# Attention's gate loads issued behind the spread reciprocals, and their bias added to x in the projection's step

## The chip, the cores and the metric

The kernel runs on one core of a Trainium2 chip. The metric is the device time in microseconds of one execution. PE is TensorE's matmul stream (PEld its weight loads), DVE is VectorE, ACT is ScalarE, POOL is GpSimd, and SP is SyncE, which here does nothing but issue DMAs. Each engine works through its own instructions in order and waits where an operand is not ready. All DMAs in the part studied here are issued on SP's queue, so a DMA that waits for its source also holds back every DMA issued behind it.

## The reference

The input x has 128 batches of 64 tokens and 128 channels, in float32. There are four blocks; only the first three use the code in question. A self-attention with 16 heads of 8 channels, its output scaled by a gate per batch and channel, is (shortened):

```python
qkv = (modulate(_ln(x), shift, scale) @ W_qkv + b_qkv)
attn = softmax(q @ k.T * HD ** -0.5)          # 16 heads, 64 x 64 per batch and head
x = x + gate[:, None] * ((attn @ v) @ W_proj + b_proj)
```

The first block (L0) runs a self-attention, a cross-attention with the context and an MLP; the second (L1) one cross-attention; the third (L2) again self-attention, cross-attention and MLP. The fourth (L3) is a small mixture of experts. A cross-attention has no gate: x = x + (attn @ v) @ W + b.

## The kernel before, in words

The 8192 tokens are cut into 16 groups of 512 (8 batches); `xs[s]` is the part of x that belongs to group s and stays in SBUF for the whole kernel. Attention is run as a hand-written software pipeline over groups: `attend` gets the list of all groups of several attentions in a row (L0 self then L0 cross, 32 in all; later L1 cross, L2 self, L2 cross, 48 in all), and `step(k)` issues one half group (4 batches) of each stage:

- `scores` (L459): 32 small matmuls into the one PSUM tile `sc`, then on DVE the row maxima `mx` (L476) and `e = sc - mx` (L478).
- `turned` (L484): transposes of e, and the exponential on ACT.
- `weighted` (L500): the product with v. Beside the 8 output channels of each head, columns of ones in `vbd` give the softmax's denominators, so the tile `o` holds outputs and sums.
- `prepare` (L377): a generator with eight parts for a coming group: loading the context c for cross-attentions (L385), the statistics, the normalization `xn` on POOL (L363), transposes, the storing of the transposed context `ctxT` in L0 cross (L411), k with its block-diagonal copy `kbd` on POOL (L435), q, v.
- `finish` (L521): a generator with four parts for a past group, which is where the change lies.

The four parts of `finish` for group j are issued in these steps: the first late in the second half step of group j+1, the second in the first half step of group j+2, the third in the second half step of group j+2, the fourth in the first half step of group j+3. They do this:

1. The denominators go to DRAM (`sums`, two DMAs, L529) and come back as a compact 128 x 64 tile (`rc`, L533). In a self-attention `gate_tile` (L272) then loads `gt` with two DMAs (L277): for each token the gate and the gate times the projection's bias, from a small table in DRAM, the row of a batch repeated for its 64 tokens. Four DMAs (L538) move the odd heads' outputs within `o`.
2. DVE takes the reciprocal of rc (L540); it goes to DRAM (`recs`, L542) and is read back spread over each head's 8 channels (`rb`, L544).
3. POOL forms `oT = o * rb` (L547) and adds the bias to x (L549): a row of biases in a cross-attention, the second half of gt in a self-attention.
4. PE projects oT (`py`, L553). In a cross-attention DVE adds py to x. In a self-attention DVE multiplies py by the first half of gt (`y`, L558), and POOL adds y to x (L559).

On each engine and on SP's queue the order is the order in which the Python code issues: in `step`, the second part of group i-2 comes before the fourth part of group i-3, and the first part of group i-1 before the third of group i-2. Tile pools with two buffers hold gt, rc and y; rb and oT have one. In the first self-attention, the `prepare` of L0 cross starts four groups before the end of the self groups, so that from then on SP also issues c, and somewhat later the stores of ctxT, between rb and the next group's sums; at the end of L2 self it is c alone.

Of the kernel before, what the change touches and what calls it, by code (L numbers as in the profile page):

```python
# [11 lines left out]
ALU = mybir.AluOpType  # L12
# [3 lines left out]
P = 128  # L16
NST = 16
TT = 4
# [41 lines left out]
def tile_kernel(ctx: ExitStack, tc: tile.TileContext, a: dict, out: bass.AP):  # L60
    nc = tc.nc
    V, S, G, T = nc.vector, nc.scalar, nc.gpsimd, nc.tensor
# [3 lines left out]
    def const(shape, name):  # L66
        return cp.tile(shape, F32, tag=name, name=name)
# [25 lines left out]
    xs = [const([P, TT, P], f"x{s}") for s in range(NST)]  # L93
# [91 lines left out]
    proj_bias = {}  # L185
# [86 lines left out]
    def gate_tile(pool, s, wp):  # L272

        gt = pool.tile([P, TT, 2, P], F32, tag="gt", name="gt")
        for h in range(2):
            r = gates[wp].rearrange("(s t h) i c -> s h t (i c)", t=TT, h=2)[s, h]
            nc.sync.dma_start(  # L277
                gt[ts(h, L)].rearrange("p t i c -> p t (i c)"),
                r.unsqueeze(0).broadcast_to([L, TT, 2 * P]),
            )  # L280
        return gt
# [239 lines left out]
    def finish(pools, at):  # L521

        pool, psum = pools[:2]
        s, o = at["s"], at["o"]
        cross = at["layer"][2] == "c"

        sums = dp.tile([16, NT], F32, tag="sums", name="sums", bufs=2)
        for j in range(2):
            nc.sync.dma_start(  # L529
                sums.rearrange("(g i j) t -> j g i t", i=2, j=2)[j], o[16 + j : P : 32, :, :]  # L530
            )
        rc = pool.tile([P, L], F32, tag="rc", name="rc")
        nc.sync.dma_start(rc, sums.rearrange("h (c t) -> (h c) t", t=L))  # L533
        if not cross:
            gt = gate_tile(pool, s, at["wp"])

        for g in range(4):
            nc.sync.dma_start(o[32 * g + 16 : 32 * g + 32, 0, :], o[32 * g : 32 * g + 16, 1, :])  # L538
        yield
        V.reciprocal(rc, rc)  # L540
        recs = dp.tile([16, NT], F32, tag="recs", name="recs", bufs=2)
        nc.sync.dma_start(recs.rearrange("h (c t) -> (h c) t", t=L), rc)  # L542
        rb = pool.tile([P, NT], F32, tag="rb", name="rb", bufs=1)
        nc.sync.dma_start(rb, recs.unsqueeze(1).broadcast_to([16, HD, NT]))  # L544
        yield
        oT = pool.tile([P, NT], F32, tag="oT", name="oT", bufs=1)
        G.tensor_tensor(oT, o[:, 0, :], rb, ALU.mult)  # L547
        bias = proj_bias[at["wp"]].unsqueeze(1).broadcast_to([P, TT, P]) if cross else gt[:, :, 1, :]
        G.tensor_tensor(xs[s], xs[s], bias, ALU.add)  # L549
        yield  # L550
        py = psum.tile([P, TT, P], F32, tag="mm", name="py")
        for t in range(TT):
            T.matmul(py[:, t, :], oT[:, ts(t, P)], w[at["wp"]][:, 0], start=True, stop=True)  # L553
        if cross:
            V.tensor_add(xs[s], xs[s], py)
        else:
            y = pool.tile([P, TT, P], F32, tag="y", name="y")
            V.tensor_tensor(y, py, gt[:, :, 0, :], ALU.mult)  # L558
            G.tensor_tensor(xs[s], xs[s], y, ALU.add)  # L559

    def attend(pools, ats):

        n = len(ats)
        prep = [prepare(pools, at) for at in ats]
        fin = [finish(pools, at) for at in ats]

        def go(gens, i):
# [708 lines left out]
```

## Time and profile before

| | |
|---|---|
| median of 3 runs | 1644.17 us (1642.24 to 1647.26) |
| the profiled execution's own time | 1646.88 us |
| its span | 1645.1 us |
| granted TensorE clock, mean | 0.996 |
| L0 self (first to last reciprocal) | about 49 to 233 us |
| L2 self (first to last reciprocal) | about 781 to 961 us |
| gate loads in attention | 64 DMAs of 256 KB |
| sums / rc / recs / rb | 160 of 16 KB / 80 of 32 KB / 80 of 32 KB / 80 of 256 KB |
| bias adds in self-attention, POOL L549 | 32 of 1278 ns |

The span is what the profiler saw between the first and the last instruction; the execution's own time is 1.8 us longer. The page gives for each group of instructions the engine, the line, the tiles as out<-in, the count, the busy time, the mean duration, and the idle time just before with what ended it. A timeline lists single instructions by start; a bracket behind one is the idle time before it and what released it.

### The profile page before, as it was taken

Reading aid. Unit: us, or ns where it says so; the run is one execution under the profiler, and the core shown is the slowest. Engines: PE = TensorE matmul, PEld = TensorE weight load, DVE = VectorE, ACT = ScalarE, POOL = GpSimd, SP = SyncE. Lnnn points to the kernel's source line nnn. Section 1 sums busy time; section 2 is a strip of 40 time slices with the busy share of each in tenths; the row PEclk is TensorE's granted clock in tenths of the full one; section 3 lists DMA queues with packets and bytes.
Section 4 is the critical chain, followed back from the end, with each engine's and each line's share of the span. In section 5 each row is a group of like instructions: output and inputs, shape, how many; then the busy total and the mean of one; then the engine's idle time right before and its main releaser. Section 6 shows DMA issues by size and latency. Waiting matters only on the chain.

```text
span 1645.1 us, 64937 instructions
## 1 busy us (share of the span) xinstructions
PE 1585.5 (96%) x27874; PEld 1094.6 (67%) x27874; DVE 1292.3 (79%) x2426; ACT 1029.8 (63%) x1696; POOL 1090.0 (66%) x1834
## 2 busy tenths in 40 slices
PE   6999999998999899999999999998999999999998
PEld 4677767776554477767777777776777666666665
DVE  7999989998576688899999999996453666666665
ACT  5788767776333587887878888885334444444442
POOL 5687777775899888977778776775866333334322
PEclk9999999999999999999999999999999999999999
DMA  7333443322202022222333432222432101111100
GB/s 207 83 95 85 104 117 89 92 80 61 61 27 59 26 60 62 61 52 56 85 91 86 109 86 73 62 59 55 127 81 74 39 30 36 39 34 38 31 13 16
DMA packets 145998, 112.70 MB, mean 69 GB/s; under 512 B 35573, under 2 KB 124463, under 8 KB 145711
## 3 DMA queue, kind: packets, MB, share of 16 engines
q1 hardware_dynamic: 145504, 108.53, 25.0%
q8 instruction: 219, 3.59, 1.0%
q14 instruction: 68, 0.56, 0.1%
q10 hardware_dynamic: 207, 0.03, 0.0%
HBM read 83.99 MB, written 14.02 MB: 60 GB/s over the span
## 4 chain that ended last, share of the span: by engine, by line
PE 75%; DVE 14%; POOL 3%; ACT 3%; DMA 2%; issue 2%; SPq 1%; POOLq 0%; DVEq 0%; ACTq 0%
PE sc L469 9%; PE pp L494 8%; PE po L511 7%; PE ph L1043 6%; PE ph L1044 6%; DVE mx L476 6%; DVE e L478 6%; PE ph L674 5%; PE po L1074 5%; PE psT L333 5%; PE pk L427 4%; PE py L553 4%; PE pvv L450 3%; PE py L691 3%; PE pq L440 3%; PE py L680 2%
## 5 line engine op out<-in xcount | busy, mean ns | idle before, releaser
L498 ACT ACTIVATE eT<-pp 128x1024 f32<-128x1024 f32 x320 | 329.6, 1030 | 165.4 <-PE pp L494 165.3
L476 DVE TENSOR_REDUCE mx<-sc 128x32 f32<-128x2048 f32 x160 | 366.5, 2291 | 59.7 <-PE sc L469 59.6
L478 DVE TENSOR_TENSOR e<-sc,mx 128x2048 f32<-128x2048 f32 x160 | 366.7, 2292 | 5.5
L494 PEld LDWEIGHTS pp<-ident,e 64*128 64x128 f32 x5120 | 185.2, 139 | 141.9 <-ACT eT L498 45.3
L435 POOL TENSOR_SCALAR kbd<-kT,mask 128x512 f32<-128x512 f32 x316 | 212.3, 689 | 38.5 <-ACT kT L429 35.6
L494 PE MATMUL pp<-ident,e 64*128 64x64 f32 x5120 | 229.0, 229 | 8.5 <-DVE e L478 4.7
L363 POOL TENSOR_SCALAR xn<-x,nmu,rs 128x128 f32<-128x128 f32 x508 | 220.0, 447 | 13.3
L547 POOL TENSOR_TENSOR oT<-o,rb 128x512 f32<-128x512 f32 x80 | 102.0, 1274 | 160.8 <-DMA rb<-recs 75.6
L469 PE MATMUL sc<-kbd,qT 32*64 32x256 f32 x5120 | 181.0, 390 | 16.5 <-DVE e L478 14.8
L675 ACT ACTIVATE h<-ph,vec 128x512 f32<-128x512 f32 x128 | 87.3, 687 | 157.8 <-PE ph L674 157.7
L511 PE MATMUL po<-eT,vbd 128*32 128x64 f32 x10240 | 178.5, 221 | 1.3 <-issue 0.8
L1050 ACT ACTIVATE h<-h 128x512 f32<-128x512 f32 x112 | 69.1, 628 | 160.0 <-DVE h L1046 131.9
L511 PEld LDWEIGHTS po<-eT,vbd 128*32 128x32 f32 x10240 | 151.8, 110 | 14.3 <-issue 1.3
L321 POOL TENSOR_TENSOR rs<-rs,nhalf 128x4 f32<-128x4 f32 x128 | 130.7, 1021 | 10.7
L469 PEld LDWEIGHTS sc<-kbd,qT 32*64 32x64 f32 x5120 | 98.2, 132 | 53.4 <-issue 19.3
L1046 DVE TENSOR_TENSOR h<-ph,ab 128x512 f32<-128x512 f32 x112 | 76.9, 687 | 64.6 <-PE ph L1044 64.4
L311 DVE BATCH_NORM_STATS2 st<-x 128x6 f32<-128x128 f32 x512 | 110.5, 279 | 1.0 <-DMA x<-in_x_dram 0.5
L1067 POOL TENSOR_SCALAR g<-g 128x512 f32<-128x512 f32 x16 | 10.0, 622 | 140.7 <-ACT g L1066 140.7
L1043 PE MATMUL ph<-nx,w 128*128 128x512 f32 x192 | 99.8, 601 | 0.0
L1074 PEld LDWEIGHTS po<-w_2o,h 128*128 128x128 f32 x768 | 92.2, 192 | 10.9 <-issue 8.4
L1079 DVE SCALAR_TENSOR_TENSOR acc<-po,pr,acc 128x128 f32<-128x128 f32 x192 | 67.2, 350 | 39.9 <-PE po L1074 35.3
L519 ACT COPY o<-po 128x512 f32<-128x512 f32 x160 | 95.7, 598 | 4.4 <-PE po L511 2.1
(259 smaller groups left out, 2954.7 us busy)
## 6 DMA issues: line engine op xcount, KB each, us to landing
rb<-recs SPq DMA_DIRECT2D x80, 256.0 KB
c<-in_ctx_dram SPq DMA_DIRECT2D x80, 256.0 KB
o<-o SPq DMA_DIRECT2D x320, 32.0 KB
gt<-gate_L_xcond_sa_proj_w SPq DMA_DIRECT2D x32, 256.0 KB
gt<-gate_L_xcond_W_proj SPq DMA_DIRECT2D x32, 256.0 KB
gt<-gate_L_xcond_W_mlp SPq DMA_DIRECT2D x32, 256.0 KB
x<-in_x_dram SPq DMA_DIRECT2D x16, 256.0 KB
ctxT<-cm SPq DMA_DIRECT2D x16, 256.0 KB
```

The source lines that it names most:

```text
L311: V.bn_stats(st[:, t, :], src[:, t, :])
L321: G.tensor_tensor(rs, rs, nhalf, ALU.pow)
L363: engine.tensor_scalar(xn[:, t, :], src[:, t, :], nmu[:, t : t + 1], rs[:, t : t + 1], ALU.add, ALU.mult)
L435: (V if at.get("first") else G).tensor_scalar(kbd[:, j], by_batch(kT), mask[:, j : j + 1], 1.0, ALU.mult, ALU.mult)
L469: T.matmul(sc[ts(h, L), g, ts(t2, 256)], qT[ts(g, 32), ts(b, L)], kbd[ts(g, 32), :, b, :], start=True, stop=True,)
L476: V.tensor_reduce(mx, sc.rearrange("p g (m k) -> p (g m) k", k=L), AX.X, ALU.max)
L478: V.tensor_tensor(e, sc.rearrange("p g (m k) -> p (g m) k", k=L), mx.unsqueeze(2).broadcast_to([P, 32, L]), ALU.subtract,)
L494: T.transpose(pp[:, h, ts(4 * g2 + 2 * i + t2, L)], e6[ts(h, L), 2 * gg + g2, t2, i], ident[ts(h, L), ts(h, L)],)
L498: S.activation(eT[:, gg], pp, AF.Exp, scale=HD ** -0.5)
L511: T.matmul(po[ts(g, 32), i, ts(2 * t2 + h, L)], at["vbd"][:, 4 * u + 2 * t2 + h, 2 * g + i, :], e7[:, g // 2, h, g % 2, i, t2, :], start=T ...
L1043: T.matmul(ps, wn, d["nx"], start=True, stop=False)
L1074: T.matmul(po[:, ex, :], d[q][:, ts(t, P)], k3["w_2o"][:, q, :], start=r == 0, stop=r == 1)
```

## The change

In self-attention groups two things move, and nothing is added or removed. The call of `gate_tile`, and with it the two DMAs of gt, moves from the first part of `finish` (behind rc, ahead of the moves within o) to the end of the second part (behind rb). The bias add on POOL moves from the third part (behind oT) to the fourth, where it is issued after the projection's matmuls and ahead of y. Cross-attentions are unchanged.

```diff
         nc.sync.dma_start(rc, sums.rearrange("h (c t) -> (h c) t", t=L))
-        if not cross:
-            gt = gate_tile(pool, s, at["wp"])
 
         for g in range(4):
...
         nc.sync.dma_start(rb, recs.unsqueeze(1).broadcast_to([16, HD, NT]))
+        if not cross:
+            gt = gate_tile(pool, s, at["wp"])
         yield
         oT = pool.tile([P, NT], F32, tag="oT", name="oT", bufs=1)
         G.tensor_tensor(oT, o[:, 0, :], rb, ALU.mult)
-        bias = proj_bias[at["wp"]].unsqueeze(1).broadcast_to([P, TT, P]) if cross else gt[:, :, 1, :]
-        G.tensor_tensor(xs[s], xs[s], bias, ALU.add)
+        if cross:
+            bias = proj_bias[at["wp"]].unsqueeze(1).broadcast_to([P, TT, P])
+            G.tensor_tensor(xs[s], xs[s], bias, ALU.add)
         yield
...
         else:
+            G.tensor_tensor(xs[s], xs[s], gt[:, :, 1, :], ALU.add)
             y = pool.tile([P, TT, P], F32, tag="y", name="y")
             V.tensor_tensor(y, py, gt[:, :, 0, :], ALU.mult)
```

## The prediction

> **What bounds the kernel now.** The page first. TensorE is busy 96% of the span, and nearly the whole chain of work that ended last runs over PE and DVE in attention. No queue heads the list, so the question is where a queue reaches into that chain.
>
> ```profile
> PE 1585.5 (96%) x27874; PEld 1094.6 (67%) x27874; DVE 1292.3 (79%) x2426; ACT 1029.8 (63%) x1696; POOL 1090.0 (66%) x1834
> PE 75%; DVE 14%; POOL 3%; ACT 3%; DMA 2%; issue 2%; SPq 1%; POOLq 0%; DVEq 0%; ACTq 0%
> ```
>
> Second, the timeline of a quiet stretch of the first self-attention (columns: start, duration, engine, line, operation).
>
> ```profile
> 157.06 0.54 DVE L540 RECIPROCAL rc<-rc 128x64 f32<-128x64 f32 x1
> 157.63 0.33 SPq L542 DMA_DIRECT2D recs<-rc  x1
> 160.93 0.56 SPq L544 DMA_DIRECT2D rb<-recs  x1
> 161.62 1.17 SPq L529 DMA_DIRECT2D sums<-o  x2
> 164.37 1.28 POOL L547 TENSOR_TENSOR oT<-o,rb 128x512 f32<-128x512 f32 x1 [2.45 <-DMA sums<-o]
> 164.78 0.33 SPq L533 DMA_DIRECT2D rc<-sums  x1
> 165.25 1.30 SPq L277 DMA_DIRECT2D gt<-gate_L_xcond_sa_proj_w  x2
> 166.60 2.50 SPq L538 DMA_DIRECT2D o<-o  x4
> 168.98 0.54 DVE L540 RECIPROCAL rc<-rc 128x64 f32<-128x64 f32 x1
> ```
>
> One group takes 11.92 us (reciprocal to reciprocal, 157.06 to 168.98). DVE sets it: twice a 2.29 us maximum and a 2.29 us subtraction, with PE's 1.12 us of scores between. The reciprocal (0.54) and y (0.63) just fill one such gap, so a reciprocal that waits for rc lengthens the group nearly one for one. SP closes a loop beside this: reciprocal, recs, rb, the next group's sums, rc, next reciprocal. Here it has slack.
>
> Third, DVE's timeline and the chain of waits later in the same stage, where SP also loads c and stores ctxT for the next layer: there the slack is gone.
>
> ```profile
> 206.59 0.55 DVE L540 RECIPROCAL rc<-rc 128x64 f32<-128x64 f32 x1 [1.19 <-DMA rc<-sums]
> 219.47 0.55 DVE L540 RECIPROCAL rc<-rc 128x64 f32<-128x64 f32 x1 [1.28 <-DMA rc<-sums]
> 233.06 0.55 DVE L540 RECIPROCAL rc<-rc 128x64 f32<-128x64 f32 x1 [1.78 <-DMA rc<-sums]
> ...
> PEld py L553 <- POOL oT L547: 5.7, 4, 2.4
> DVE rc L540 <- DMA rc<-sums: 5.0, 4, 1.8
> ```
>
> The reciprocals stand at 192.82, 206.59, 219.47, 233.06 and 245.85: 53.0 us for four groups instead of 47.7. These 5.3 us are nearly all that SP's order can win.
>
> **The change, part by part.**
>
> *Bias add on POOL.* The 32 adds of 1.28 us (40.9 us busy) stay, later in POOL's order: removed between oT and the two rs operations, placed between kbd and the add of y. Behind the old place rs moves up 1.28 us; behind the new one the add of y, nmu and four xn slip by as much, then oT. Kbd ends near 158.7; two adds of 1.28 and 1.9 us of nmu and xn end at about 163.2, while oT waits for rb until 164.37 anyway (the 2.45 us idle). xn is read a group later, x by the next layer sixteen groups later. Cost zero; the cover is that idle time. Without it (126.44, oT idle only 0.47) oT slips up to 1.28, PE's py still has more than that in hand, and the price is at most a few tenths.
>
> *The two gate DMAs.* Their bytes (0.52 MB a group) and number are unchanged; they leave the place between rc and the o moves and go behind rb. What leaves: 1.3 to 2.3 us of SP issue ahead of the o moves, and the gate's data ahead of recs. Readers of gt (the bias add and y of the fourth part) come about 12.4 us after the reciprocal, gt lands by about 9 (issued at 3 to 5, and the lone load below takes 3.8 from issue to its last data): no wait. What arrives: behind gt on SP now stand c, ctxT and, above all, the next sums, on which rc and the DVE reciprocal depend. The work on DVE, PE and ACT is untouched.
>
> How long does gt hold the rings? Nearest row: the windows of one gate load alone, in the last MLP.
>
> ```profile
> 1268.00:1268.50 0.50, 0.50 (x17) 0.43 (x13) 0.00 (x0) 0.00 (x0) 0.00 (x0) 1.00 0.19 68
> 1268.50:1269.00 0.50, 0.50 (x2) 0.26 (x3) 0.43 (x2) 0.00 (x0) 0.00 (x0) 1.00 0.95 336
> 1269.00:1270.00 1.00, 1.00 (x8) 0.76 (x7) 0.42 (x1) 0.36 (x1) 0.00 (x0) 1.00 1.11 234
> 1270.00:1271.00 1.00, 1.00 (x6) 0.66 (x6) 0.00 (x0) 0.33 (x1) 0.00 (x0) 1.00 0.48 89
> ```
>
> The last two columns are DMA share and GB/s: about 2.5 us of data. The Trainium skill (DMA: Bandwidth & Descriptors, "Anatomy of one DMA — SWDGE (gpsimd) path") puts data at bytes over 436e3 per us behind about 2 us of fixed cost, for another issue path: 1.2 us for 0.52 MB. I take the row for the rings. The price of gt ahead of sums then lies between 1.3 (issue alone) and 2.5 us in a full queue.
>
> The SP loop afterwards, from one reciprocal's start to the next:
> - to recs: 0.57 (157.06 to 157.63).
> - recs to rb: 1.5 to 3.3 before; by the queue's timeline the mean is 2.4 in groups with gates and 2.0 in L1 cross, which has none. Gates now come later: 2.0.
> - rb to issue of rc: not shown with gt in it; bounded below by 3.85 (160.93 to 164.78, no gt), above by 3.85 + 2.5. The nearest row has the same 0.77 MB behind rb's start: rb, c and ctxT at 198.12, rc at 203.75, so 5.6. Taken.
> - rc to the reciprocal it releases: 2.84, 1.85 and 2.28 (rc at 203.75, 217.62, 230.78): 2.3.
>
> Sum 10.5, against 11.92: in the mean hidden, slack 1.4. The parts scatter by about 0.9 us together (estimate from the ranges above), so a group now and then overshoots; the mean overshoot is some 0.05 us. By kind of group:
> - 20 groups with no load in their way (ten in each self-attention): 20 x 0.05 = +1.0.
> - Six at the end of the second self-attention and two in the first, with c: 0.8 more, 11.3; overshoot about 0.13: +1.0.
> - Four with c and ctxT: 0.6 + 2.3 (o moves still right ahead of recs) + 5.7 + 2.0 for gt (between 1.3 and 2.5) + 2.3 = 12.9, against 53.0/4 = 13.26: -1.4. What wins here is that recs no longer stands behind gt and o moves (reciprocal 206.59, recs only 209.08, rb 212.04); what eats it is gt ahead of sums. With the page's 1.2 us of data the issue's 1.3 would set the term, the loop would be 12.2 and the four groups would win 4.2.
>
> Sum +0.6 us: 1647.5 against the profiled execution's own 1646.88 (span 1645.1 plus 1.8 around it). That execution lies 2.7 us above the median of the three runs, so against 1644.17 it is 1644.8. With the page's figure it would be about 1642.
>
> **The rivals.** *Slower: the reciprocal waits for gates.* One mechanism: gt ahead of sums on SP and in the rings, paid at the DVE reciprocal. It decides from the point where rb to rc exceeds 7.0 us, because then the quiet loop passes 11.92. At 7.1 (1.5 more than taken) the quiet groups have about 0.4 us each (8), the eight with c about 0.9 (7), the four late ones 14.4 against 13.26 (4.6): +20, 1664. At half that excess, about +7, 1651. For: rc already waits late in the first self-attention with no gt in the way, gate issues stretch from 1.3 to 2.3 us, gate rows are small pieces read many times. Against: the quiet loop's 1.4 us.
>
> *Faster: the late groups come free.* If recs lands in 1.5 and gt costs only its issue, the late loop is 0.6 + 1.5 + 7.0 + 1.9 = 11.0, below 11.92, and the 5.3 us go: 1638.9. For: PE's 5.7 us of waiting on oT there comes from a late rb, and rb moves up. Against: rb, gt, c and ctxT are then 1.3 MB in a row, with sums behind them.
>
> *Nothing happens at all:* the bias half is that; the DMA half would be if the waits just change places. It is inside the main case.
>
> **How the numbers follow.** About 0.3% (4.9 us) is what a measurement of this kernel can tell from no change. Main case, loops as summed: 0.50, of which 0.39 within the bound, 0.04 faster, 0.07 slower (each part is a small difference of large terms). Slower rival 0.34: 0.29 slower, 0.05 within. Faster rival 0.16: 0.13 faster, 0.03 within. Together: faster 0.17, same 0.47, slower 0.36. Range: from the faster rival's 1638 to between the slower one's half and full price, 1657; the main case's own is 1640 to 1650.
>
> **What would show it.** Right: in quiet stretches sums starts about 0.4 us later after the reciprocal than 4.56 now, rc to reciprocal shrinks from 4.2–4.9 us towards 3, without a DVE wait for rc; recs to rb falls towards 2.0; late in the first self-attention recs follows the reciprocal within about 0.6–1 us instead of 2.5, rb to rc grows from 5.7 to about 7.7, the period there is about 12.9; oT's wait for rb does not grow. Wrong: DVE waits for rc in most of the 32 groups (slower rival); no DVE wait for rc late in the first self-attention (faster); a wait of y or of the bias add for gt; oT or xn late because of POOL's new order.

## The result and the profile after

The changed kernel takes 1657.15 us (median of 6 runs, 1655.15 to 1660.71) against 1643.33 for the kernel before in the same series (1640.6 to 1647.26): ratio 1.0084, 95% interval 1.0066 to 1.0103. It is slower by about 14 us, where the forecast's likeliest case was no change. The profiled execution of after has a span of 1655.4 us, 10.3 more than before's 1645.1. The traces can explain these 10.3 us; the rest of the 13.8 is that before's profiled execution lay above its own median.

The page of after: busy times as before, but more of the chain runs through DMA.

```profile
PE 1585.6 (96%) x27874; PEld 1094.1 (66%) x27874; DVE 1292.3 (78%) x2426; ACT 1031.3 (62%) x1696; POOL 1091.0 (66%) x1834
PE 74%; DVE 14%; DMA 4%; ACT 3%; POOL 3%; issue 2%; SPq 1%; POOLq 0%; DVEq 0%; ACTq 0%
```

No engine works more than 1.5 us longer (PE 1585.5 before, 1585.6 now); the DMA share of the chain went from 2% to 4%. So the loss is waiting. The same quiet stretch as was shown of before, by the timeline (start, duration, engine, line, operation; the lines have shifted with the edit: L538 is the reciprocal, L540 recs, L542 rb, L529 sums, L533 rc):

```profile
159.16 0.54 DVE L538 RECIPROCAL rc<-rc 128x64 f32<-128x64 f32 x1
159.73 0.33 SPq L540 DMA_DIRECT2D recs<-rc  x1
162.62 0.56 SPq L542 DMA_DIRECT2D rb<-recs  x1
163.23 1.30 SPq L277 DMA_DIRECT2D gt<-gate_L_xcond_sa_proj_w  x2
164.64 1.15 SPq L529 DMA_DIRECT2D sums<-o  x2
169.12 0.32 SPq L533 DMA_DIRECT2D rc<-sums  x1
171.32 0.55 DVE L538 RECIPROCAL rc<-rc 128x64 f32<-128x64 f32 x1 [0.16 <-DMA rc<-sums]
```

From rb to rc it is 6.50 us here (before: 3.85), and of that the sums' own round trip, from their issue to rc's, is 4.48 (before, 161.62 to 164.78: 3.16). The slack is used up: the bracket shows DVE beginning to wait for rc.

SP's own waits over the first ten groups (49 to 170 us) say the same. Before, then after (total us, times, longest):

```profile
SPq L533 <- DMA sums<-o: 13.9, 11, 1.8
SPq L529 <- ACT qT L442: 13.6, 9, 2.4
...
SPq L533 <- DMA sums<-o: 24.9, 11, 3.0
SPq L529 <- ACT qT L442: 5.4, 6, 1.9
```

On average SP waits 1 us longer for sums to land before it can issue rc. The second row shows something else: in quiet groups sums does not start as soon as rb is issued, but when ACT has copied o (the row names qT, which ACT runs right behind that copy). In before this was about 4.5 us after the reciprocal, whether rb had come 1.5 or 3.3 us after recs. So an earlier rb gains nothing on the way to rc in a quiet group. The issue of the gates mostly falls into that wait, and what they add shows in the time from sums to rc.

Where SP also loads c the loop no longer fits. DVE's timeline in the stretch that follows, and the whole run's row in the chain of waits (total us, times, longest):

```profile
184.94 0.55 DVE L538 RECIPROCAL rc<-rc 128x64 f32<-128x64 f32 x1 [1.78 <-DMA rc<-sums]
199.78 0.55 DVE L538 RECIPROCAL rc<-rc 128x64 f32<-128x64 f32 x1 [3.24 <-DMA rc<-sums]
212.62 0.54 DVE L538 RECIPROCAL rc<-rc 128x64 f32<-128x64 f32 x1
225.83 0.55 DVE L538 RECIPROCAL rc<-rc 128x64 f32<-128x64 f32 x1 [0.40 <-DMA rc<-sums]
239.35 0.55 DVE L538 RECIPROCAL rc<-rc 128x64 f32<-128x64 f32 x1 [1.90 <-DMA rc<-sums]
252.36 0.55 DVE L538 RECIPROCAL rc<-rc 128x64 f32<-128x64 f32 x1 [1.41 <-DMA rc<-sums]
...
DVE rc L538 <- DMA rc<-sums: 21.2, 12, 3.5
```

Before, that row read 12.2 us in 6 waits; now it is 21.2 in 12. In the two self-attentions alone it is 5.0 us in 4 waits before and 14.3 in 10 after; 8 of these 10 are in the 12 groups where c is also loaded. The chain of after through the longest of these waits shows what stands in it, one SP instruction behind the other (L277 the two gate loads, L385 c; pieces under 0.1 us are left out):

```profile
189.83 0.56 SPq L542
...
190.45 0.64 SPq L277
...
191.14 0.61 SPq L277
...
191.79 0.60 SPq L385
...
193.11 4.04 DMA sums<-o
...
197.20 2.49 DMA rc<-sums
```

The two gate issues take 1.3 us, and the second of the two 16 KB DMAs of sums behind them takes 4.04 us to land. In the group of the same place before, sums was issued 1.29 us after rb and rc 3.23 us after sums; here it is 2.66 and 4.71. The gates' issue and their data are both paid in one group.

A second loss was not foreseen. Three quiet groups lasted 12.88, 13.10 and 12.88 us without any DVE wait for rc. PE's timeline there shows a gap in the middle of a run of matmuls whose operands were ready, put down to no releaser:

```profile
108.73 0.60 PE L554 MATMUL py<-L_xcond_sa_proj_w,oT 128*128 128x128 f32 x3 [0.70 <-issue]
143.88 0.42 PE L511 MATMUL po<-eT,vbd 128*32 128x64 f32 x14 [0.90 <-issue]
879.35 0.53 PE L511 MATMUL po<-eT,vbd 128*32 128x64 f32 x21 [0.69 <-issue]
```

The same stretches of before have none of these. The most likely cause is PE's supply of instructions, for this reason. DMA queue 8, which the page calls `instruction`, brings blocks of 16 KB (219 of them, 3.59 MB), in the self-attentions one every 5.2 us in the median. In all the traces of this case together there are 33 gaps of PE's matmuls of over 0.3 us that have no releaser, and every one of them ends 1.2 to 1.6 us after such a block has landed. The three gaps above followed blocks that came 7.1, 6.9 and 7.7 us after the one before. The windows in which the block before the gap at 143.88 came show it at the end of the burst of rb and gt (the last two columns are the DMA share, where 1 is all 16 engines, and GB/s):

```profile
141.00:141.50 0.50, 0.50 (x21) 0.14 (x6) 0.23 (x4) 0.36 (x1) 0.50 (x1) 1.00 0.67 131
141.50:142.00 0.50, 0.50 (x16) 0.44 (x15) 0.47 (x1) 0.00 (x0) 0.33 (x3) 1.00 0.12 35
```

In the self-attentions of after ten blocks come over 6.5 us behind the last one, in before and in the kernel without gate loads none. That PE waits for a block in these gaps is thus well supported by the timing. That gt's burst is what delays the block is argued; gaps of about 1.0 to 1.2 us also stand in traces of kernels whose gates had not been moved (the bias add alone, c and ctxT on ScalarE's queue).

Stage by stage, from reciprocal to the same reciprocal in both traces:

| stage | before | after | difference | forecast |
|---|---|---|---|---|
| L0 self, ten quiet groups | 119.49 | 121.87 | +2.4 | +0.5 |
| L0 self, two with c | 23.84 | 28.46 | +4.6 | +0.25 |
| L0 self, four with c and ctxT | 53.03 | 52.58 | -0.45 | -1.4 |
| L2 self, ten quiet groups | 119.20 | 121.92 | +2.7 | +0.5 |
| L2 self, six with c | 73.73 | 75.95 | +2.2 | +0.75 |

The sum is +11.5, of which about 1.2 comes back later (the spans differ by 10.3). Of the quiet groups' 5.1 the three gaps make 3.1 (12.88, 13.10 and 12.88, each less 11.92), and one group of L2 that overshoots (a 1.34 us wait for rc) most of the rest. One of the four late groups (from 199.78) also holds a short drop of the granted TensorE clock, 0.57 in the mean from 201.5 to 205.5, where before has 1.00 in all of both self-attentions; it lasted 12.84 us without a wait for rc, so the -0.45 is not the DMAs' order alone.

### The profile page after: what moved, and what is told of

Read it like the earlier page. It is cut to its first block, busy times and chain, and to the rows that moved or that the text cites. A ratio compares the mean times of both kernels' runs of the same rounds, so it can differ in the third digit from the quotient of the medians.

```text
span 1655.4 us, 64995 instructions
## 1 busy us (share of the span) xinstructions
PE 1585.6 (96%) x27874; PEld 1094.1 (66%) x27874; DVE 1292.3 (78%) x2426; ACT 1031.3 (62%) x1696; POOL 1091.0 (66%) x1834
## 3 DMA queue, kind: packets, MB, share of 16 engines
q8 instruction: 219, 3.59, 0.9%
## 4 chain that ended last, share of the span: by engine, by line
PE 74%; DVE 14%; DMA 4%; ACT 3%; POOL 3%; issue 2%; SPq 1%; POOLq 0%; DVEq 0%; ACTq 0%
PE sc L469 8%; PE pp L494 8%; PE po L511 6%; PE ph L1045 6%; PE ph L1046 6%; DVE e L478 6%; DVE mx L476 6%; PE ph L676 5%; PE po L1076 5%; PE psT L333 5%; PE pk L427 4%; PE py L554 4%; PE py L693 3%; PE pvv L450 3%; PE pq L440 3%; PE py L682 2%
## 5 line engine op out<-in xcount | busy, mean ns | idle before, releaser
L547 POOL TENSOR_TENSOR oT<-o,rb 128x512 f32<-128x512 f32 x80 | 102.0, 1275 | 125.8 <-DMA rb<-recs 57.3
```

## The experiments

Two theories stood at the start. A: the gate loads' new place costs everything, since they stand ahead of sums. B: POOL's new order, with the bias add moved, costs. All ratios below are against the kernel before on the same chip in the same series (medians 1644.1 for the first four kernels, 1645.6 for the next four, 1646.19 for the last four), with 95% intervals.

### One part at a time

*Only the gate loads moved* (against the kernel before):

```diff
-        if not cross:
-            gt = gate_tile(pool, s, at["wp"])
...
         nc.sync.dma_start(rb, recs.unsqueeze(1).broadcast_to([16, HD, NT]))
+        if not cross:
+            gt = gate_tile(pool, s, at["wp"])
```

> Only the gate loads move behind rb; the bias add stays behind oT in the third part. Theory A (gates ahead of sums on SP and in the rings, paid as DVE waits for rc and as PE gaps): all of the loss is here, 1654 to 1661 us, with DVE waits for rc in the groups that also load c; POOL's bias add may now wait for gt for up to 2 us a group, hidden or adding a few us. Theory B (the loss comes from POOL's new order: y's add, nmu, xn and oT late): near the kernel before, 1641 to 1647.

Measured: 1656.22 us, ratio 1.0073 (1.0059 to 1.0086). POOL's bias add did wait for gt, 44.5 us over the 32 groups and up to 2.6 us each, and yet the time is that of the changed kernel: these waits are hidden.

*Only the bias add moved* (against the kernel before):

```diff
-        bias = proj_bias[at["wp"]].unsqueeze(1).broadcast_to([P, TT, P]) if cross else gt[:, :, 1, :]
-        G.tensor_tensor(xs[s], xs[s], bias, ALU.add)
+        if cross:
+            bias = proj_bias[at["wp"]].unsqueeze(1).broadcast_to([P, TT, P])
+            G.tensor_tensor(xs[s], xs[s], bias, ALU.add)
...
         else:
+            G.tensor_tensor(xs[s], xs[s], gt[:, :, 1, :], ALU.add)
             y = pool.tile([P, TT, P], F32, tag="y", name="y")
             V.tensor_tensor(y, py, gt[:, :, 0, :], ALU.mult)
```

> Only the bias add moves to the fourth part; the gate loads stay behind rc. Theory A: as the kernel before within 3 us, 1641 to 1647, reciprocal periods of 11.92 in quiet groups. Theory B: 1652 or more.

Measured: 1643.63 us, ratio 0.9997 (0.9989 to 1.0005). The loads' move has all the loss and the bias add's has none. B falls. In this trace the four late groups took 50.4 us and not 53.0, so the 5.3 us that the prediction read from one profiled execution of before are not there in full every time.

### The floor

*After, with 56 of the 64 gate loads left out:*

```diff
-            gt = gate_tile(pool, s, at["wp"])
+            if s < 2:
+                kept_gt[s] = gate_tile(pool, s, at["wp"])
+            gt = kept_gt[s % 2]
```

> The changed kernel, but each self-attention loads the gates of its first two groups only and reuses those tiles for all others, so 28 x 2 + 0 of the 64 gate loads are left out (the gates of later groups are the wrong ones). Theory A: neither SP nor rings are held, so no DVE wait for rc and no PE gap without a releaser in self-attention; also the late groups of before, about 5 us, are won: 1635 to 1641. Theory B: POOL's order is that of the changed kernel, so 1650 or more.

Measured: 1639.87 us, ratio 0.9975 (0.9963 to 0.9986). With the loads away, DVE waits for rc in no self-attention group, PE's quiet stretches have no gap, and the late groups run 12.03 us each. So what the gate loads cost at their old place is about 4 us, and another place could win that much at most; the prediction's 5.3 us for the late groups was near this.

### Other places on the same queue

*In the first part, but behind the moves within o* (against after):

```diff
         for g in range(4):
...
+        if not cross:
+            gt = gate_tile(pool, s, at["wp"])
         yield
...
-        if not cross:
-            gt = gate_tile(pool, s, at["wp"])
```

> Bias add in the fourth part as in the changed kernel, gate loads in the first part, but behind the four moves within o instead of ahead of them: off the path from rb to sums. Theory A: near the kernel before, 1641 to 1648; the late groups change little, because recs again stands behind gt. If it is the mere distance of gt from rc or oT that costs, 1652 or more.

Measured: 1671.27 us, ratio 1.0169 (1.015 to 1.0187): a miss, and the worst of the places tried on this queue. Sums to rc falls to mostly 2.6 to 3.4 us, as expected of a queue without gt ahead of sums; but now recs stands right behind gt. From recs to rb it is mostly 3.5 to 5.0 us instead of 2.4, rb is late, and oT starts mostly 8.3 to 10.5 us after the reciprocal (before: 5.5 to 7.4 in quiet groups). The chain of waits shows PE paying:

```profile
PEld py L554 <- POOL oT L547: 46.6, 37, 3.8
PE py L554 <- POOL oT L547: 19.7, 17, 3.0
```

Before, the first of these rows was 13.7 us in 17 waits and the second 2.2 in 3. Here it is recs that pays for standing right behind the burst, as sums does in the changed kernel.

*One gate DMA behind rc, the other behind rb* (against after; `gate_tile` takes the halves to load):

```diff
+        if not cross:
+            gt = gate_tile(pool, s, at["wp"], (0,))
         for g in range(4):
...
-            gt = gate_tile(pool, s, at["wp"])
+            gate_tile(pool, s, at["wp"], (1,), gt)
```

> Bias add in the fourth part; one of the two gate DMAs stays behind rc, the other goes behind rb, so each place has 256 KB. By the data theory half a burst is hidden at the new place (e6) and recs has half the burst ahead: no DVE waits for rc in quiet groups, the late groups of L0 self a little faster: 1639 to 1645. If the number of SP issues ahead of sums counts: about half the loss, 1648 to 1652.

Measured: 1655.28 us, ratio 1.0059 (1.0041 to 1.0077): a miss. In the first self-attention recs to rb is again 3 to 4 us in most groups, and in the four late groups rc is waited for up to 4.2 us: each half is paid by its follower. In the ten quiet groups of L2, though, the two halves did fit: recs to rb is mostly 1.5 to 1.9 us and no reciprocal waits for rc; the waits return with c.

*Between recs and rb, where SP waits for recs to land anyway* (against after):

```diff
         nc.sync.dma_start(recs.rearrange("h (c t) -> (h c) t", t=L), rc)
+        if not cross:
+            gt = gate_tile(pool, s, at["wp"])
         rb = pool.tile([P, NT], F32, tag="rb", name="rb", bufs=1)
         nc.sync.dma_start(rb, recs.unsqueeze(1).broadcast_to([16, HD, NT]))
-        if not cross:
-            gt = gate_tile(pool, s, at["wp"])
```

> Bias add in the fourth part; both gate DMAs between recs and rb, where SP waits 1.5 to 3.3 us for recs anyway. By the loop's sum the burst starts 1.5 to 2 us earlier than behind rb, so rc has its slack back, and rb lands 1 to 2 us later, which py just allows (oT at 7.5 to 8.5 us after the reciprocal, needed by 8.6): 1640 to 1647. If recs or rb is held as in e4 (oT past 9 us): 1655 or more.

Measured: 1643.98 us, ratio 0.9988 (0.9982 to 0.9994). The interval lies below 1, though the gain is smaller than the 0.3% that one comparison of this kernel can tell; against the changed kernel it is 13 us. SP's timeline late in the first self-attention, then DVE's:

```profile
207.29 0.33 SPq L540 DMA_DIRECT2D recs<-rc  x1
207.66 1.33 SPq L277 DMA_DIRECT2D gt<-gate_L_xcond_sa_proj_w  x2
209.36 0.54 SPq L544 DMA_DIRECT2D rb<-recs  x1
209.99 0.54 SPq L385 DMA_DIRECT2D c<-in_ctx_dram  x1
210.62 1.65 SPq L411 DMA_DIRECT2D ctxT<-cm  x1
212.36 1.17 SPq L529 DMA_DIRECT2D sums<-o  x2
215.68 0.32 SPq L533 DMA_DIRECT2D rc<-sums  x1
```
```profile
194.69 0.54 DVE L538 RECIPROCAL rc<-rc 128x64 f32<-128x64 f32 x1
206.72 0.54 DVE L538 RECIPROCAL rc<-rc 128x64 f32<-128x64 f32 x1
218.78 0.54 DVE L538 RECIPROCAL rc<-rc 128x64 f32<-128x64 f32 x1
```

The issue of gt fills time in which SP would have waited: recs to rb is 2.07 us here, although both gate DMAs stand between. The DMA behind the burst is rb, whose reader, oT, has some slack. There is no bracket for rc, and the late groups take 12.0 to 12.1 us each, where before took 12.8 to 13.8. It does not reach the floor: three quiet groups still take 12.8 to 13.1 us. PE waits for a late oT in one of them (oT 9.6 us after the reciprocal), has a gap without a releaser in the second (0.76 us), and waits for ACT's copy of o in the third (0.98 us).

### Issue or data

*After, same number of gate DMAs at the same place, half the bytes:*

```diff
-            gt = gate_tile(pool, s, at["wp"])
+            gt = pool.tile([P, TT, 2, P], F32, tag="gt", name="gt")
+            for h in range(2):
+                r = gates[at["wp"]].rearrange("(s t h) i c -> s h t i c", t=TT, h=2)[s, h][:, 0, :]
+                nc.sync.dma_start(gt[ts(h, L), :, 0, :], r.unsqueeze(0).broadcast_to([L, TT, P]))
...
-            G.tensor_tensor(xs[s], xs[s], gt[:, :, 1, :], ALU.add)
+            G.tensor_tensor(xs[s], xs[s], gt[:, :, 0, :], ALU.add)
```

> The changed kernel with half the bytes a gate load: the same two DMAs with the same number of rows, but only the gate and not gate times bias is loaded, and the gate is added in the bias's place (that part of the result is left out). Data theory: the loss falls to well under half, 1643 to 1649, rb to rc about 5.3 in quiet groups, nearly no DVE waits for rc in the groups with c. Queue-order theory with the issue time as its price: SP holds sums as long as before, 1654 to 1660.

Measured: 1643.06 us, ratio 0.9986 (0.9978 to 0.9994). The whole loss is gone, while the issue is still 1.56 us in a group with c. SP's timeline of a group with c:

```profile
183.58 1.56 SPq L547 DMA_DIRECT2D gt<-gate_L_xcond_sa_proj_w  x2
185.19 0.60 SPq L385 DMA_DIRECT2D c<-in_ctx_dram  x1
185.89 1.14 SPq L529 DMA_DIRECT2D sums<-o  x2
189.12 0.33 SPq L533 DMA_DIRECT2D rc<-sums  x1
```

The gates still take 1.56 us of SP, but sums to rc is 3.23 us, where after had 4.71 in the group of the same place; quiet groups are near 2.6, and their PE gaps are gone. So the bytes of gt in front of sums decide whether the loop fits. SP's time is not free: with half the bytes rb to rc is still 6.2 to 6.5 us in the groups with c (about 5.0 without gate loads), most of it because sums starts later. But that fits into the slack, except for one wait of 3.1 us in the last of the late groups.

*After, gates issued on ScalarE's queue:*

```diff
-            gt = gate_tile(pool, s, at["wp"])
+            gt = gate_tile(pool, s, at["wp"], nc.scalar)
```

> The changed kernel with attention's gate loads issued by ACT on its own DMA queue, at the same place of the program. Queue-order theory (what costs is that sums is issued and served behind gt on SP's queue): SP is free again, rb to rc falls from 6.1 to about 4.9 us in quiet groups, 1640 to 1648 us. Data theory (what costs is the 0.5 MB burst in the shared DMA engines between rb and sums, whoever issues it): 1652 to 1660, rb to rc stays near 6. ACT's own 1.3 us of issue a group may add up to 3 us in either case.

Measured: 1688.02 us, ratio 1.0257 (1.024 to 1.0273). Neither theory had this, and the run cannot decide between them. No self-attention group waits for rc, and rb to rc fell to about 5.2 us. But the gates were also moved in time: ACT issues them 2.4 to 3.0 us before the reciprocal, where SP in the changed kernel issues them 2.7 to 5.5 us behind it, so their burst no longer stands in front of sums. And nearly every group of self-attention now takes 13.47 us. ACT's queue, then ACT, DVE and PE in one group, and the row of the chain of waits that grew:

```profile
113.76 1.25 ACTq L277 DMA_DIRECT2D gt<-gate_L_xcond_sa_proj_w  x2
115.06 0.69 ACT L429 ACTIVATE kT<-pk,vec 128x512 f32<-128x512 f32 x1 [0.89 <-PE pk L427]
116.14 0.54 DVE L538 RECIPROCAL rc<-rc 128x64 f32<-128x64 f32 x1
116.61 0.63 DVE L560 TENSOR_TENSOR y<-py,gt 128x512 f32<-128x512 f32 x1
117.29 0.66 PE L333 MATMUL psT<-ident,xn 128*128 128x128 f32 x4 [1.20 <-DVE y L560]
119.10 2.29 DVE L476 TENSOR_REDUCE mx<-sc 128x32 f32<-128x2048 f32 x1 [1.87 <-PE sc L469]
...
PE psT L333 <- DVE y L560: 44.1, 30, 1.5
```

In this kernel PE's transposes of xn (`psT`) wait for y, the scores stand behind psT on PE, and the next maximum on DVE waits for the scores. In before, psT started ahead of y (108.77 against 109.64 in one group). The row stands in no other run, and its 44.1 us are about the whole loss of 42. ACT's issue of 1.25 us delays kT, but kT ended at 115.75, 1.5 us before psT started, so it is not what psT waits for. The edit names neither psT nor y; why the built program ties them together is open.

*After, gates issued on POOL's queue:*

```diff
-            gt = gate_tile(pool, s, at["wp"])
+            gt = gate_tile(pool, s, at["wp"], nc.gpsimd)
```

> The changed kernel with attention's gate loads issued by POOL on its own queue at the same place of the program. SP is free and sums is not behind gt in its queue: by e5 rb to rc falls to about 5.2 us, and what remains is POOL's issue time, which has about 2 us of slack a group where ACT had none: 1641 to 1650. If POOL's issue takes over 2 us a group, or the data holds sums from any queue: 1655 or more.

Measured: 1649.04 us, ratio 1.0024 (1.0015 to 1.0033). Rb to rc is mostly 3.5 to 4.0 us in quiet groups and no self-attention group waits for rc. But here too the gates come at another time: POOL issues them 0.6 to 3.1 us before the reciprocal and they have landed before sums is issued, so that this is not a test of the queue alone. Their data runs beside recs, whose time to rb rises to 2.0 to 3.9 us in quiet groups and 2.9 to 5.2 with c. PE has gaps without a releaser here too:

```profile
PE po L511 <- issue: 4.2, 4, 1.9
```

### The other loads in the queue

*c and ctxT on ScalarE's queue, in after and in before:*

```diff
-            nc.sync.dma_start(c, ctx_d[s])
+            nc.scalar.dma_start(c, ctx_d[s])
...
-                nc.sync.dma_start(ctxT[s], kv_in)
+                nc.scalar.dma_start(ctxT[s], kv_in)
```

> The changed kernel with the loads of c in attention and the stores of ctxT moved from SP's queue to ACT's, so that only gt stands between rb and sums on SP. If the loss sits in the groups that also load c (by the trace 8 to 9 of its 12 us, as DVE waits for rc): 1645 to 1650, and what is left is the quiet groups' PE gaps of about 1 us each. If the data of c rather than its place on SP's queue counts: 1653 or more.

Measured, on after: 1649.6 us, ratio 1.0024 (1.0014 to 1.0035), within the first of its forecasts.

> The kernel before with the same move of c and ctxT to ACT's queue. If the late groups of L0 self are held by SP's full queue, their 5 us come free: 1637 to 1641. If they are held by the data in the rings, or ACT's issue time of 0.6 us a DMA costs as much: 1642 to 1648.

Measured, on before: 1649.18 us, ratio 1.0023 (1.0013 to 1.0033), a little above both of its forecasts. With c and ctxT out of SP's queue the two kernels take the same time, which fits a collision of gt with c in front of sums. But the move raises the kernel before by itself, and with c moved, the self-attentions of after still have 8.6 us of waits for rc in 7 places; so the pair does not settle how much of the loss needs c.

*The burst alone, in a layer that has no gates:* two gate loads that nobody reads, behind rb in L1 cross, in the kernel before.

```diff
         nc.sync.dma_start(rb, recs.unsqueeze(1).broadcast_to([16, HD, NT]))
+        if at["layer"] == "L1c":
+            gate_tile(pool, s, "L0_xcond_sa_proj_w")
```

> The kernel before plus, in the 16 groups of L1 cross, two gate loads of 256 KB behind rb into a tile that nobody reads. There the reciprocal has about 2.9 us more slack than in self-attention and oT does not wait for rb. If the PE gaps without a releaser come from a burst of rb and gt holding up PE's own instruction blocks: several gaps of about 1 us appear in L1 cross with no DVE wait for rc, 1647 to 1654 us. If those gaps have nothing to do with the burst: no change, 1641 to 1647. If the sums chain itself is over its slack even here: DVE waits for rc appear, 1650 or more.

Measured: 1657.02 us, ratio 1.0071 (1.0057 to 1.0086). L1 cross had no wait for rc before. Now DVE's timeline there reads:

```profile
623.34 0.55 DVE L540 RECIPROCAL rc<-rc 128x64 f32<-128x64 f32 x1 [1.30 <-DMA rc<-sums]
...
689.04 0.55 DVE L540 RECIPROCAL rc<-rc 128x64 f32<-128x64 f32 x1 [2.96 <-DMA rc<-sums]
```

Loads were added there and none was moved, so the burst in front of c and sums is enough by itself to make the wait. The run also says how much needs c: of the ten reciprocals that follow a burst with c behind it eight waited, but none of the six at the end of the layer, where the burst stands in front of sums without c (sums to rc 3.3 to 4.2 us). There the burst alone still fits. This run was also meant to show PE's gaps apart from the waits; it shows one (0.76 us at 786.22, in the last group), which is too little to tell.

## Why the prediction was wrong, by its own steps

- *The step that failed* is the term from rb to the issue of rc, and most of all what it becomes where c stands behind gt. It was taken at 5.6 us in a quiet group, from one group of before with the same 0.77 MB behind rb. It measured 6.2 on average (5.85 to 6.97), so that the slack was 0.8 and not 1.4. With one c it was taken 0.8 higher, 6.4; it measured 6.9 to 7.4 in L2 and 8.61 and 7.37 in L0. The kernel without gate loads shows the same term without gt: 4.6 us in quiet groups and about 5.0 in the others. So gt costs 1.6 us in a quiet group, inside the 1.3 to 2.5 that the prediction had bounded, but 2.3 to 3.0 where c stands behind it: there SP has little or no wait for o left in which to issue the gates, so that sums both starts later and lands more slowly. The prediction had issue and data as the two ends of a range, and there they add up.
- *The eight groups with c* therefore did not fit into 12 us; they lasted 11.5 to 15.4: +6.8 us where +1.0 was summed. This is the largest error.
- *The four late groups* were taken at 7.7 from rb to rc and measured 7.95: close. Their gain was 0.45 us and not 1.4. Recs followed the reciprocal in 1.4 us on average and not in 0.6 (an rc that is itself late puts its o moves late, and they stand ahead of recs as before); recs to rb and rc to the reciprocal were 0.8 us shorter than summed, which made up for most of it.
- *The quiet groups* had about 1.5 us of overshoot, near the 1.0 that was summed, but 3.1 us more from the PE gaps, which no step of the prediction had.
- *The saving in recs to rb* (2.4 to 2.0 us) was booked in full. In quiet groups it is worth nothing, since sums waits for o until about 4.5 us after the reciprocal.
- *The slower rival* had the mechanism and the place: gt ahead of sums, paid at the DVE reciprocal. Its point of decision, 7.0 us, was passed in nearly all groups with c and in no quiet one. Its price for the eight groups with c, 7 us, is what they cost (6.8). That the result as a whole lies between its half and its full price (+7 and +20) is in part luck: its 4.6 us in the late groups did not come, and 3.1 us of PE gaps, which it did not have, did.
- *Right*: the bias add costs nothing; recs to rb is about 2.0 in quiet groups; rc to the reciprocal it releases is 2.25 on average (1.6 to 3.5; 2.3 taken); y never waits for gt; oT's waiting for rb went down (75.6 to 57.3 us on POOL).
- *The row and the page*: with the Trainium skill's figure (DMA: Bandwidth & Descriptors, "Anatomy of one DMA — SWDGE (gpsimd) path"), which is for another issue path, gt would have been an estimated 1.2 us of data, hidden under its own issue of 1.3, and halving the bytes should have changed nothing. It took the loss away. The measurement decides for the row's 2.5 us.

## What to carry to other kernels

In this kernel a large load in a shared queue was paid by the short DMA right behind it that some engine awaits, so ask of each candidate place which DMA follows, who reads it and with how much slack. The best place found here is one where the issuing engine waits for a landing anyway, between recs and rb: the issue is free there and the burst falls in front of a reader with slack. An experiment that moves loads to another engine's queue moves them in time as well, since that engine has its own work in front of them: look when they are issued before reading the queue from the result. A slack worked out from one group's row is to be tested at the groups with the most in the queue, since it is there that it runs out first.

## What the hardware showed that was not expected

- Sums of 16 KB behind two gate loads of 256 KB on one queue needed mostly 3.4 to 5.0 us until rc could be issued, instead of mostly 2.55; with half the bytes, about 2.6 in quiet groups. A 32 KB recs behind the same burst needed 3.5 to 5.0 us to rb instead of 2.4.
- Issuing one gate load cost the issuing engine 0.6 us, on SP, ScalarE and POOL alike.
- PE paused up to 1.9 us in the middle of ready matmuls in many of the kernels whose DMA traffic had been moved. All 33 such gaps of over 0.3 us end 1.2 to 1.6 us after a 16 KB block of the instruction queue has landed; what makes a block late, no run isolates.
